# Who requests the weights: moving five of six weight loads of a recurrent layer from SyncE's queue to ScalarE's

## Chip, core and metric

The kernel runs on one core of a Trainium2 chip. The metric is the device time of one execution in microseconds (us). TensorE is called PE here, VectorE DVE, ScalarE ACT, GpSimd POOL and SyncE SP, as in the profile. Each of these engines takes its instructions from a queue of its own, in order. A DMA is requested by an instruction in one of those queues.

## The reference

The input is x, 2048 rows of 512 numbers. Each row is normalized (LN). A recurrent layer with 16 heads of 128 and an FFN with signs as weights both work on it, and one gates the other. What matters here, cut down:

```python
xn = _layernorm(x)
q = _silu(xn @ Wq); k = _silu(xn @ Wk); v = _silu(xn @ Wv); z = xn @ Wz
a = xn @ Wa; b = xn @ Wb
q, k, v = _causal_dwconv(q, conv_q_w), _causal_dwconv(k, conv_k_w), _causal_dwconv(v, conv_v_w)
q = q * cos + rot_half(q) * sin; k = k * cos + rot_half(k) * sin
q, k = (each divided by its norm, by head)
for s in range(4):                      # lags
    attn = einsum('bshd,bshd->bsh', q, lag(k, s)) * scale
    out = out + (attn * sigmoid(lag(a, s) * b))[..., None] * lag(v, s)
s = (out * rms * norm_w * _silu(z)) @ Wout
hidden = relu((xn @ sign(up).T) * up_scale)
g = _silu((hidden @ sign(down).T) * down_scale * output_scale)
return x + s * g
```

Wq, Wk, Wv and Wz are 512 x 2048, Wout is 2048 x 512, all float32. No weight stays in the chip's memory: each block of rows loads all of them again, by heads.

## The kernel before

**Tiles.** The 2048 rows are four blocks b of 512 tokens (NTB = 4), and the 16 heads are eight pairs p (NP = 8). A product (q, k, v or z of one pair in one block) multiplies a weight tile of 512 x 256 (512 KB, `load`, lines 301 to 304) with the block's transposed rows xnT, as two halves j of four matmuls each (`project`, 349 to 363). It takes 6.87 us on PE. ACT applies Silu to each half while copying it out of PSUM. `convolve` then starts with a scaling on ACT and goes on with three multiply-adds a half on DVE. The output projection takes two pairs at a time: four chunks of 128 tokens, `po`, from oz (the gated output) and wo (`output_projection`, 616 to 639).

**Steps.** `step(p, b)` (663 to 739) does the products q and k of block b + 1 and the products v and z of block b for one pair. An opening stage runs `step(p, -1)`: q and k of block 0, mixed with the first block of the FFN. Then come 24 steps with b = 0, 1 and 2, each about 35.3 us long. The last block's v and z and the other blocks' FFN follow.

**What crosses a block.** Over the pairs of a block, `sum_dots` and `sum_squares` collect the dots of q and k for each lag in PSUM. When a new block begins (p = 0, here called a change of block), `norms`, `norms_in_rows` (rows rq and rk, by SP) and `coefficients` make the factors from them. SP stores them in memory (`co_dram`) and fetches them back per pair, copied to 64 partitions a head: the tiles bc of `weighted` (569 to 605). DVE multiplies v with them (te), adds the lags up, and multiplies with z (oz, `gated_output`, line 607).

**What sets the order.** A scheduler places instructions by estimated costs, except for those issued through `pe`, `dve`, `act` or `sp`: these are proxies of class `InOrder` (68 to 78), which keep the order of the program among themselves on their engine. All their instructions bear line 76 in the profile. `nc.scalar` and `nc.sync` are free to be moved. `loads["by"]` in `load` and `load_wo` (556 to 559) is SP's queue through this stage.

**Buffers.** A pool gives a tile the slot of the tile `bufs` back, and the request for the new tile waits until the old one's readers are done. q's and k's weights take turns in three slots (pool `qks`, tag "w"), v's and z's in three others (pool `vs`), and wo in three. bc has three, oz three, PSUM's `mm` six banks.

**Where the requests stand before.** q's weight is requested at the head of `queries` (392 to 399), k's at the head of `products` (from 416), v's just ahead of its product in `step` (line 688), z's at 711 or 719 and wo's at 720. All are on SP, in one queue with the rows of x and of the norm, co_dram and bc. SP can run ahead of the products as far as the slots allow.

Of the kernel before, what the change touches and what calls it, by code (L numbers as in the profile page):

```python
# [44 lines left out]
P = 128  # L45
# [8 lines left out]
NP = H // 2  # L54
TB = 512
NTB = S // TB
# [25 lines left out]
def recurrent_layer(ctx: ExitStack, tc: tile.TileContext, a: dict, out: bass.AP):  # L82
# [3 lines left out]
    pool = InOrder(tc, nc.gpsimd)  # L86
    act = InOrder(tc, nc.scalar)

    sp = InOrder(tc, nc.sync)
    loads = {"by": nc.sync}  # L90
# [207 lines left out]

    weights = {}

    def load(pool, n, p, b):
        w = pool.tile([P, KC, 2 * P], F32, tag="w", name=f"w{n}{p}_{b}", bufs=3)
        loads["by"].dma_start(w, a[f"w{n}"][p])
        weights[n] = w

    def with_halo(pool, name, tag, bufs, p, b):

# [23 lines left out]
    def first_product(to, second_half):  # L331

        pps = [mm.tile([P, TB], F32, tag="mm", name=f"pq{j}_0_0") for j in range(2)]
        for lo in range(0, TB, TB // 2):
            for j in range(2):
                for k in range(KC):
                    pe.matmul(
                        pps[j][:, lo : lo + TB // 2],
                        weights["q"][:, k, j * P : (j + 1) * P],
                        xnT[:, k, HALO + lo : HALO + lo + TB // 2],  # L340
                        start=(k == 0),
                        stop=(k == KC - 1),
                    )
                if lo == j == 0:
                    second_half()
        for j in range(2):
            (nc.scalar if j else act).activation(to[:, j, :], pps[j], AF.Silu)

    def project(n, p, b, to):
        if n == "q" and p == b == 0:  # L350
            first_product(to, second_half)
            return
        for j in range(2):
            pp = mm.tile([P, TB], F32, tag="mm", name=f"p{n}{j}_{p}_{b}")
            for k in range(KC):
                pe.matmul(
                    pp,
                    weights[n][:, k, j * P : (j + 1) * P],
                    xnT[:, k, HALO + b * TB : HALO + (b + 1) * TB],
                    start=(k == 0),  # L360
                    stop=(k == KC - 1),
                )
            nc.scalar.activation(to[:, j, :], pp, AF.Silu)  # L363

    def raw_of(pool, n, p, b, bufs=2, raw=None):

# [24 lines left out]

    def queries(p, b):

        if p or b:
            load(qks, "q", p, b)
        q = qks.tile([P, LAGS, 2, TB], F32, tag="q", name=f"q_{p}_{b}", bufs=1)
        q0 = q[:, LAGS - 1]
        convolve(0, p, raw_of(qks, "q", p, b), q0)
        return q
# [16 lines left out]
    def products(p, b, q, between=None, beside_k=None):  # L416

        n = f"_{p}_{b}"
        if p or b:
            load(qks, "k", p, b)  # L420
        q0 = q[:, LAGS - 1]
        raw = raw_of(qks, "k", p, b)
        if p == 0:
            sum_squares(p)
        k = sum_with_halo(qks, "k", p, b)
        convolve(1, p, raw, k[:, :, HALO:])
        if between:
            between()
        turn(q)

        sq = [qks.tile([P, 2, TB], F32, tag=f"sq{j}", name=f"sq{j}" + n, bufs=3 - 2 * j) for j in range(2)]
        for j in range(2):
            act.activation(sq[j][:, 0], q0[:, j], AF.Square)
            act.activation(sq[j][:, 1], k[:, j, HALO:], AF.Square)
        nc.gpsimd.dma_start(sq[0], sq[1], accum_op=ALU.add)
        squares_due.append((p, sq[0]))
        if beside_k:
            beside_k()

        def product(to, j, lo, hi):  # L440

            k0 = k[:, j, lo : lo + TB]
            k_lags = bass.AP(k0.tensor, k0.offset, [k0.ap[0], [1, hi - lo], k0.ap[1]])
            dve.tensor_tensor(to, q[:, lo:hi, j, :], k_lags, ALU.mult)

        pr = qks.tile([P, LAGS, TB], F32, tag="pr", name="pr0" + n, bufs=2)
        product(pr, 0, 0, LAGS)
        if not b or p % 2 == 0:
            pr1 = qks.tile([P, LAGS, TB], F32, tag="pr", name="pr1" + n, bufs=2)
            product(pr1, 1, 0, LAGS)  # L450
            if b:
                nc.gpsimd.dma_start(pr, pr1, accum_op=ALU.add)
            elif p < NP - 1:
                dve.tensor_tensor(pr, pr, pr1, ALU.add)
        else:

            product(q[:, :, 1], 1, 0, LAGS)
            dve.tensor_tensor(pr, pr, q[:, :, 1], ALU.add)
        if not b:

            prs = [pr, pr1] if p == NP - 1 else [pr]
            dots_due.append([p, prs, of_head[:, p], p == NP - 1, True])
            return


        for h in range(0, P, D // 2):
            first, second = slice(h, h + D // 4), slice(h + D // 4, h + D // 2)
            if p % 2 == 0:
                nc.gpsimd.dma_start(pr[first], pr[second], accum_op=ALU.add)
            else:  # L470
                both = dots_due[-1][1][0]
                nc.gpsimd.dma_start(both[second], pr[first])
                nc.gpsimd.dma_start(both[second], pr[second], accum_op=ALU.add)
        if p % 2 == 0:
            dots_due.append([p, [pr], of_heads[:, p // 2], p == NP - 2, False])
        else:
            dots_due[-1][-1] = True
# [75 lines left out]

    wos = {}

    def load_wo(p, b):
        wo = vs.tile([P, 2, HID], F32, tag="wo", name=f"wo_{p}_{b}", bufs=3)
        loads["by"].dma_start(wo, a["wo"][p])
        wos[p] = wo

    def gates_of_output(p, b):
# [101 lines left out]
    def step(p, b, beside_q=None, beside_k=None):  # L663
# [21 lines left out]
        if z_due:  # L685
            z_due.pop()()
        if at:
            load(vs, "v", p, b)
            raw = raw_of(vs, "v", p, b, 1, rv)
        if first_due:  # L690
            first_due.pop()()
# [16 lines left out]

        early = p == 2 and b == 0
        if early:  # L710
            load(vs, "z", p, b)
            z_of()

        output_projections(strips if p % 2 == 0 or due else None)
        if change:
            coefficients(b)
        if at:
            if not early:
                load(vs, "z", p, b)
            load_wo(p, b)  # L720
            out_of = lambda: gated_output(p, b, weighted(p, b, v), z[0])
            if change:
                z_due.append(z_of)
                first_due.append(out_of)
            else:
                if not early:
                    z_of()
                out_of()
# [66 lines left out]
    with tc.tile_pool(name="pre", bufs=1, side="right") as pre:  # L795
# [64 lines left out]
        for p in range(NP):  # L860
# [9 lines left out]
            if p + 2 < NP:  # L870
                fetch(*groups[p + 2])
    vs = att.enter_context(tc.tile_pool(name="vs", bufs=1, side="right"))
    for b in range(NTB - 1):
        for p in range(NP):
            step(p, b)
# [12 lines left out]
    raw = raw_of(vs, "v", 1, last, 1)  # L888
    load(vs, "v", 2, last)
    load_wo(0, last)  # L890
    z_weights = {0: weights["z"]}
    load(vs, "z", 1, last)
    z_weights[1] = weights["z"]
    output_projections(sum_dots, 1)
    coefficients(last)
    qk.close()
# [15 lines left out]
        return up[:, f].rearrange("p (k m) -> p k m", k=KC)  # L912


    v_weights = {}
    for p in range(NP + 1):
        if 1 < p < NP:
            weights["v"] = v_weights.pop(p)
            raw = raw_of(vs, "v", p, last, 1)
        if p:  # L920
            weights["z"] = z_weights.pop(p - 1)
            z = gates_of_output(p - 1, last)
        squares_of_o()

        if p % 2 == 1 and p != 3 or p == 4:
            output_projections()
        if 1 < p < NP:
            load(vs, "z", p, last)
            z_weights[p] = weights["z"]
        if 0 < p < NP:  # L930
            v = values(p, last, raw)
        if p and p + 2 < NP:
            load(vs, "v", p + 2, last)
        if p + 2 < NP:
            v_weights[p + 2] = weights["v"]
        if p:
            gated_output(p - 1, last, o, z)
        if p < NP:
            o = weighted(p, last, v)
        if p == 4:  # L940
            load_wo(3, last)
        if 0 < p < NP and p != 3:
            load_wo(p, last)

        if p < NP:
            some = slice(2 * p, 2 * p + 2)
            pool.dma_start(up[:, some], signs_dram["up"][:, some])
        else:
            pool.dma_start(first_down, signs_dram["down"][:, 0:NFD])
        if p == 4:  # L950
            xs = in_two_terms(ffw, tokens(1), "xs", 1, [P, KC, TB], "xs1")
        elif 4 < p < 7:
            for b in range(last):
                load_squares(b, p - 5)
        elif p == NP:
            load_squares(last, 0)
            load_squares(last, 1)
# [8 lines left out]
    with tc.tile_pool(name="ff", bufs=1, side="right") as ff:  # L966
# [75 lines left out]
        for b in range(1, NTB):  # L1042
            pf = [mm.tile([P, HID], F32, tag="mm", name=f"pf{c}_{b}") for c in range(TC)]
            for f in range(2, NFC + 2):
                ub, uf = (b, f) if f < NFC else (b + 1, f - NFC)
                if uf == 0 and ub < NTB:
                    xs = ahead
                if ub < NTB:

                    ph = (mm, mm, sums, sums)[uf % 4].tile(  # L1050
# [12 lines left out]
                if b > 1 and f < 2 + TC:  # L1063
                    gate(f - 2)
                if f == NFC - 4 and b + 1 < NTB:
                    ahead = in_two_terms(
                        ff if b == 1 else ffw, tokens(b + 1), "xs", 1, [P, KC, TB], f"xs{b + 1}"
                    )
                if b == last and f >= NFC - 3:
# [105 lines left out]
```

## Time and profile before

| what | before |
|---|---|
| median of 3 timed runs | 1400.17 us (1399.67 to 1402.85) |
| the profiled execution | 1400.38 us |
| its span (first to last instruction) | 1398.6 us |
| granted TensorE clock | 0.998 |
| busy: PE / DVE / ACT / POOL | 1387.6 / 1179.3 / 671.3 / 236.1 us |
| a weight's request on SP at line 303 (32 wq, 32 wk, 24 wv, 24 wz), shortest / median | 0.327 / 0.329 to 0.384 us |
| one of 128 bc requests on SP, shortest / median / longest | 0.573 / 0.600 / 2.267 us |
| memory traffic | 263.4 MB, mean 188 GB/s |

The span is the time between the first and the last instruction in the profile. The execution's own time is 1.8 us longer. A busy time counts an engine's computing instructions; DMA requests are not in it, and stand in rows of their own (SPq is SP's queue). "Granted clock" is the share of full speed that TensorE was allowed. A wait in the profile's list of waits names the instruction that waited, and behind the arrow what ended its wait last. The opening stage ends at about 198 us, the 24 steps end at about 1018 us.

### The profile page before, as it was taken

The page shows a single profiled execution, that of the slowest core. Times are in us where ns is not written, and L with a number is a line of the kernel's source. Part 1 is how long each engine was busy: PE and PEld are TensorE (multiplying, and loading weights), DVE is VectorE, ACT ScalarE, POOL GpSimd, SP SyncE. Part 2 cuts the span into 40 slices and gives each one's busy share as a digit, 9 for nine tenths or more (in the row PEclk, how much of TensorE's full clock was granted, in tenths as well). Part 3 has the DMA queues.
Part 4 walks back from the last instruction along what each step waited for, and adds up shares of the span by engine and source line. Part 5 has one row for each costly group of instructions (what it writes and reads, how often), then busy time and mean ns, then how long its engine had stood idle before and what let it go on. Part 6 is the DMA issues. An engine that isn't in the chain of part 4 may idle for free.

```text
span 1398.6 us, 12500 instructions
## 1 busy us (share of the span) xinstructions
PE 1387.6 (99%) x3962; PEld 689.6 (49%) x3962; DVE 1179.3 (84%) x1183; ACT 671.3 (48%) x1309; POOL 236.1 (17%) x317
## 2 busy tenths in 40 slices
PE   9999999999999999999999999999999999999998
PEld 6555544444444444444444444444444444578886
DVE  7998989999898989998999999989884987337454
ACT  7566656546454564565545544545442433222122
POOL 2222111112213121113131112111111122200000
PEclk9999999999999999999999999999999999999999
DMA  9979577888988789889986897888849999654020
GB/s 315 332 171 211 129 200 166 228 203 197 231 199 186 167 167 242 212 211 196 212 186 159 171 251 186 207 181 182 176 92 207 262 233 237 142 204 136 24 90 30
DMA packets 104985, 263.40 MB, mean 188 GB/s; under 512 B 17812, under 2 KB 18324, under 8 KB 100568
## 3 DMA queue, kind: packets, MB, share of 16 engines
q0 software_dynamic: 36672, 108.02, 40.0%
q1 hardware_dynamic: 68248, 154.58, 37.1%
q8 instruction: 32, 0.52, 0.2%
q14 instruction: 33, 0.27, 0.1%
HBM read 159.77 MB, written 52.45 MB: 152 GB/s over the span
## 4 chain that ended last, share of the span: by engine, by line
PE 87%; DVE 7%; DMA 3%; ACT 1%; issue 1%; SPq 0%; DVEq 0%; ACTq 0%
PE pq L76 14%; PE pk L76 14%; PE po L76 14%; PE pz L76 13%; PE pv L76 12%; PE ph L76 8%; PE pf L76 8%; DVE q L76 2%; DVE te L76 2%; DMA wk<-in_wk_dram 1%; DVE v L76 1%; PE dots L76 1%; DMA bc<-co_dram 1%; PE squares L76 1%; DVE k L76 1%
## 5 line engine op out<-in xcount | busy, mean ns | idle before, releaser
L76 PE MATMUL pq<-xnT,wq 128*128 128x512 f32 (+1 forms) x528 | 226.1, 580 | 0.6 <-ACT rk L310 0.6
L76 PE MATMUL pk<-xnT,wk 128*128 128x512 f32 x512 | 225.3, 592 | 0.8 <-DMA wk<-in_wk_dram 0.8
L76 PE MATMUL pz<-xnT,wz 128*128 128x512 f32 x512 | 225.2, 592 | 0.5 <-ACT rv L363 0.5
L76 PE MATMUL po<-wo,oz 128*128 128x512 f32 x512 | 225.6, 595 | 0.0
L76 PE MATMUL pv<-xnT,wv 128*128 128x512 f32 x512 | 225.2, 592 | 0.0
L76 DVE TENSOR_TENSOR te<-v,bc 128x2048 f32<-128x2048 f32 x64 | 143.8, 2288 | 33.8 <-ACT v L76 15.8
L76 DVE SCALAR_TENSOR_TENSOR k<-rk,conv_w,k 128x512 f32<-128x512 f32 x192 | 141.7, 751 | 31.6 <-ACT k L375 27.1
L76 PEld LDWEIGHTS pq<-xnT,wq 128*128 128x128 f32 x528 | 99.0, 189 | 123.4 <-issue 115.1
L76 PEld LDWEIGHTS po<-wo,oz 128*128 128x128 f32 x512 | 96.2, 190 | 126.5 <-issue 117.1
L76 PEld LDWEIGHTS pz<-xnT,wz 128*128 128x128 f32 x512 | 96.6, 189 | 124.0 <-issue 119.2
L76 PEld LDWEIGHTS pv<-xnT,wv 128*128 128x128 f32 x512 | 96.6, 189 | 123.8 <-issue 120.2
L76 PEld LDWEIGHTS pk<-xnT,wk 128*128 128x128 f32 x512 | 96.5, 189 | 121.7 <-issue 119.6
L76 DVE SCALAR_TENSOR_TENSOR q<-rq,conv_w,q 128x512 f32<-128x512 f32 x192 | 141.5, 749 | 17.4 <-ACT q L375 10.6
L76 DVE SCALAR_TENSOR_TENSOR v<-rv,conv_w,v 128x512 f32<-128x512 f32 x192 | 141.3, 750 | 6.4 <-ACT v L375 1.9
L76 DVE SCALAR_TENSOR_TENSOR q<-q,turns 128x1024 f32<-128x1024 f32 (+1 forms) x128 | 127.3, 1015 | 4.9 <-ACT q L76 2.6
L76 DVE TENSOR_TENSOR pr<-q,k 128x2048 f32<-128x2048 f32 x52 | 117.3, 2287 | 0.9
L76 DVE CAST hid_hi<-hid 128x512 fp32r<-128x512 f32 x52 | 22.4, 430 | 89.7 <-ACT hid L785 89.7
L785 ACT ACTIVATE hid<-ph,up_scale 128x512 f32<-128x512 f32 x64 | 43.6, 685 | 108.6 <-PE ph L76 108.0
L363 ACT ACTIVATE rq<-pq 128x512 f32<-128x512 f32 x62 | 36.9, 596 | 98.2 <-PE pq L76 98.1
L633 ACT COPY part<-po 128x512 f32<-128x512 f32 x64 | 37.0, 580 | 87.8 <-PE po L76 87.7
L76 PE MATMUL ph<-xs_hi,up 128*128 128x512 f32 x192 | 76.8, 400 | 0.0
L76 PE MATMUL ph<-xs_lo,up 128*128 128x512 f32 x192 | 75.6, 394 | 0.0
(154 smaller groups left out, 1747.2 us busy)
## 6 DMA issues: line engine op xcount, KB each, us to landing
bc<-co_dram SPq DMA_DIRECT2D x128, 256.0 KB
pr<-pr POOLq DMA_DIRECT2D x72, 256.0 KB, 6.9
wq<-in_wq_dram SPq DMA_DIRECT2D x32, 512.0 KB
wk<-in_wk_dram SPq DMA_DIRECT2D x32, 512.0 KB
sq<-sq POOLq DMA_DIRECT2D x32, 512.0 KB, 6.7
wv<-in_wv_dram SPq DMA_DIRECT2D x32, 512.0 KB
wz<-in_wz_dram SPq DMA_DIRECT2D x32, 512.0 KB
wo<-in_wo_dram SPq DMA_DIRECT2D x32, 512.0 KB
```

Of the source, the lines that this page charges most:

```text
L76: return self.tc.keep_in_program_order(getattr(self.engine, op)(*args, **kwargs))
L363: nc.scalar.activation(to[:, j, :], pp, AF.Silu)
L633: nc.scalar.copy(part, po)
L785: nc.scalar.activation(hid, ph, AF.Relu, scale=scale)
```

## The change

The requests for q, k, v, z and wo in the 24 steps move from SP's queue to ACT's.

- The weights are kept by name, pair and block. `load` and `load_wo` take the engine that requests.
- A list, `ahead`, has all q and k weights of blocks 1 to 3 in order of use, and another all v and z weights of blocks 0 to 2. After the opening stage SP requests the first three of each.
- In `project`, after both halves of a product (and so behind its second Silu in ACT's program order), ACT requests the next of the same list. This is the weight of the product three further on in the same pool, and it goes into the slot that the product just done has left.
- wo is requested by ACT at the place in `step` where SP did it.
- The opening stage, the last block's v, z and wo, the rows of x, bc and everything else stay on SP. `ahead` at line 1066 becomes `next_xs` because the name is taken.

In the changed program PE's and DVE's instructions stand in the same order as before. SP has 114 requests fewer and ACT as many more. Some ACT instructions change places: at a change of block the squares of q and their copies come earlier, copies of halos later.

```diff
-    def load(pool, n, p, b):
+    def load(pool, n, p, b, by=None):
         w = pool.tile([P, KC, 2 * P], F32, tag="w", name=f"w{n}{p}_{b}", bufs=3)
-        loads["by"].dma_start(w, a[f"w{n}"][p])
-        weights[n] = w
+        (by or loads["by"]).dma_start(w, a[f"w{n}"][p])
+        weights[n, p, b] = w
+
+    ahead = {
+        "qk": [(n, p, b) for b in range(1, NTB) for p in range(NP) for n in "qk"],
+        "vz": [(n, p, b) for b in range(NTB - 1) for p in range(NP) for n in "vz"],
+    }
+
+    def load_ahead(pool, kind, by=None):
+        if ahead[kind]:
+            load(pool, *ahead[kind].pop(0), by)
...
     def project(n, p, b, to):
...
             nc.scalar.activation(to[:, j, :], pp, AF.Silu)
+        weights.pop((n, p, b))
+        if n in "qk" and b:
+            load_ahead(qks, "qk", act)
+        elif n in "vz" and b < NTB - 1:
+            load_ahead(vs, "vz", act)
...
     def queries(p, b):
 
-        if p or b:
+        if p and not b:
             load(qks, "q", p, b)
...
     def products(p, b, q, between=None, beside_k=None):
...
-        if p or b:
+        if p and not b:
             load(qks, "k", p, b)
...
-    def load_wo(p, b):
+    def load_wo(p, b, by=None):
         wo = vs.tile([P, 2, HID], F32, tag="wo", name=f"wo_{p}_{b}", bufs=3)
-        loads["by"].dma_start(wo, a["wo"][p])
+        (by or loads["by"]).dma_start(wo, a["wo"][p])
...
         if at:
-            load(vs, "v", p, b)
             raw = raw_of(vs, "v", p, b, 1, rv)
...
         if early:
-            load(vs, "z", p, b)
             z_of()
...
         if at:
-            if not early:
-                load(vs, "z", p, b)
-            load_wo(p, b)
+            load_wo(p, b, act)
...
     vs = att.enter_context(tc.tile_pool(name="vs", bufs=1, side="right"))
+    for _ in range(3):
+        load_ahead(vs, "vz")
+        load_ahead(qks, "qk")
     for b in range(NTB - 1):
         for p in range(NP):
             step(p, b)
```

More of the change, by code (lines that the diff above doesn't have):

```diff
@@ L338, in first_product @@
                         pps[j][:, lo : lo + TB // 2],
-                        weights["q"][:, k, j * P : (j + 1) * P],
+                        weights["q", 0, 0][:, k, j * P : (j + 1) * P],
                         xnT[:, k, HALO + lo : HALO + lo + TB // 2],
@@ L357, in project @@
                     pp,
-                    weights[n][:, k, j * P : (j + 1) * P],
+                    weights[n, p, b][:, k, j * P : (j + 1) * P],
                     xnT[:, k, HALO + b * TB : HALO + (b + 1) * TB],
@@ L890, in recurrent_layer @@
     load_wo(0, last)
-    z_weights = {0: weights["z"]}
     load(vs, "z", 1, last)
-    z_weights[1] = weights["z"]
     output_projections(sum_dots, 1)
@@ L912, in up_of @@
         return up[:, f].rearrange("p (k m) -> p k m", k=KC)
-    v_weights = {}
     for p in range(NP + 1):
         if 1 < p < NP:
-            weights["v"] = v_weights.pop(p)
             raw = raw_of(vs, "v", p, last, 1)
         if p:
-            weights["z"] = z_weights.pop(p - 1)
             z = gates_of_output(p - 1, last)
@@ L928, in recurrent_layer @@
             load(vs, "z", p, last)
-            z_weights[p] = weights["z"]
         if 0 < p < NP:
@@ L933, in recurrent_layer @@
             load(vs, "v", p + 2, last)
-        if p + 2 < NP:
-            v_weights[p + 2] = weights["v"]
         if p:
@@ L1046, in recurrent_layer @@
                 if uf == 0 and ub < NTB:
-                    xs = ahead
+                    xs = next_xs
                 if ub < NTB:
@@ L1065, in recurrent_layer @@
                 if f == NFC - 4 and b + 1 < NTB:
-                    ahead = in_two_terms(
+                    next_xs = in_two_terms(
                         ff if b == 1 else ffw, tokens(b + 1), "xs", 1, [P, KC, TB], f"xs{b + 1}"
```

## The prediction

> **What bounds the kernel now.** I read the page first: the busy times, the span in slices and the chain that ended last.
>
> ```profile
> PE 1387.6 (99%) x3962; PEld 689.6 (49%) x3962; DVE 1179.3 (84%) x1183; ACT 671.3 (48%) x1309; POOL 236.1 (17%) x317
> PE   9999999999999999999999999999999999999998
> DMA  9979577888988789889986897888849999654020
> PE 87%; DVE 7%; DMA 3%; ACT 1%; issue 1%; SPq 0%; DVEq 0%; ACTq 0%
> ```
>
> The profiled run took 1400.38 us: a span of 1398.6 and 1.8 outside it; the median of the three timed runs is 1400.17, so the two agree and I sum against 1400.4. TensorE (PE) is busy for 1387.6 us, which leaves 11.0 us idle. Next I asked what PE waited for:
>
> ```profile
> PE pf L76 <- DVE hid_lo L76: 0.9, 1, 0.9
> PE pk L76 <- DMA wk<-in_wk_dram: 0.8, 1, 0.8
> PE pq L76 <- ACT rk L310: 0.6, 1, 0.6
> PE pz L76 <- ACT rv L363: 0.5, 1, 0.5
> ```
>
> Columns: total us, times, longest. A single wait, 0.8 us, is for a weight. That row is the whole prize. The others are for the vector engines (rows of the opening stage, the last block), whose code the change leaves alone. Windows confirm it: in the stage it touches, from 195 to 1070 us, PE works 874.2 of 875 us.
>
> ```profile
> 195.00:1070.00 875.00, 874.20 (x2198) 376.01 (x2197) 806.67 (x750) 448.36 (x901) 158.15 (x198) 1.00 0.84 194
> ```
>
> Columns: length, then busy us of PE, weight load, DVE, ACT, POOL; clock, DMA share, GB/s. VectorE (DVE) is the second bound: 875 - 806.67 = 68.3 us idle over some 24.8 steps of 35.3 us, 2.75 us a step. ScalarE (ACT) is half idle. DMA works 84%.
>
> **What is removed.** SP loses 114 requests: 90 of q, k, v, z and 24 of wo. Its waits show what it does there:
>
> ```profile
> SPq L303 <- PE pq L76: 110.4, 22, 13.0
> SPq L303 <- PE pv L76: 91.3, 15, 11.6
> SPq L558 <- PE po L76: 123.3, 11, 14.5
> ```
>
> These are waits for a slot that PE is still reading. While SP stands in one, everything queued behind it on SP stands too: bc rows, x, the next weight. That is idle time of a queue, and nobody on PE's path notices but once. The one case, from SP's timeline and the chain that ended last:
>
> ```profile
> 308.40 0.33 SPq L303 DMA_DIRECT2D wk<-in_wk_dram  x1
> ```
>
> ```profile
> 308.40 20.25 DMA wk<-in_wk_dram
> 328.79 7.11 PE pk L76 x16
> ```
>
> The weight of pair 4, block 1 was requested at 308.40, landed 20.25 us later, and PE started 0.8 us late. After the change ACT requests it behind the second Silu of the product three back in its pool, pq of pair 3; in ACT's timeline that Silu ends at 301.15, some 7 us sooner. If the weight takes as long again, it lands at about 321.4, ahead of 328.0, when PE wanted it. **-0.8 us.**
>
> Here the skill speaks against any gain: "DMA: Bandwidth & Descriptors", section "Issuing engines are not separate DMA queues", says that DMAs from scalar, sync and gpsimd share the same 16 engines, so that issuing from several saves only the time to initiate, usually small. By that rule the gain is one issue, 0.33 us, and 0.5 of the wait remains. By the row it is the earlier slot, not the issue, and all 0.8 goes. I take the row; the ends are 0.3 and 0.8.
>
> The same number of buffers (three to a pool) limits the lead before and after. Elsewhere weights land at least 4.6 us ahead of their product, so being earlier there is worth nothing. At nothing too stand SP's six requests at the start of the stage, the keyed dictionary and the renaming; PE's and DVE's instruction orders are identical, POOL's differs by a few neighbours.
>
> **What is added on ACT.** 114 requests, 4.75 a step. No ACT-issued DMA is in the trace. SP's own rows bound it: a weight's request takes 0.33 us alone, about 0.55 after others, and 1.4 to 2.5 under backlog (2.54 for wq at 315.34). Below zero it cannot be. I take 0.55, as ACT's requests come one at a time, with 63 us in all; ACT's share in the stage goes from 51% to 58%. A request also waits for its slot and for the DMA eight back in the two queues' shared set of completion semaphores (the built program shows these waits); nearly always both are past by then. The slot is the product's own reads, done before its Silu.
>
> Queued behind each q, k or v request is the scaling that opens the same product's convolution, and DVE waits for that. The DVE waits "k <- ACT k" are 27.1 us in 15 times and "q <- ACT q" 10.6 in 7 in the whole span, so DVE is up against ACT in about one product in four. If all three requests of a step were on DVE's path, they would cost 3 x 0.55 = 1.65 us, inside the 2.75 that it has. Behind DVE stands PE: PSUM banks are freed by ACT's Silu some 8 to 19 us before PE needs them (typically 16), so 0.55 there is nothing. wo's request waits on po of the step before last, also past. **In the ordinary steps: 0.**
>
> If that cover is gone, the thin places are where po needs the last oz: 2.4 us at 279.4, 2.3 at 344.3, and, thinnest, at the two later changes of block: 1.04 us at 557.7 (oz ends at 556.67, po's third matmul starts 555.99 + 4 x 0.43) and 1.42 at 841.8. There DVE runs without a gap for over 20 us:
>
> ```profile
> 547.26 4.49 DVE L76 TENSOR_TENSOR te<-v,bc 128x2048 f32<-128x2048 f32 x2 [0.18 <-ACT xnT L76]
> 551.79 2.29 DVE L76 TENSOR_TENSOR te<-te,te 128x2048 f32<-128x2048 f32 x1
> 555.45 1.22 DVE L76 TENSOR_TENSOR oz<-te,z 128x1024 f32<-128x1024 f32 x1
> ```
>
> te waits for ACT's square (0.18), and the change puts three requests (v, z, q) ahead of that square: 3 x 0.55 = 1.65 less the 0.5 or so that ACT idles ahead of them, 1.2 us later. In return ACT's new order has the other squares earlier and some halo copies later, and lets DVE start 0.7 to 0.85 sooner (my reading of the order against the durations). Net 0.4 later, inside 1.04.
>
> **What else meets at these changes.** SP's queue before:
>
> ```profile
> 511.51 0.33 SPq L539 DMA_DIRECT2D co_dram<-rk  x1
> 519.04 7.59 SPq L76 DMA_DIRECT2D bc<-co_dram  x6
> 526.67 1.41 SPq L303 DMA_DIRECT2D wv<-in_wv_dram  x1
> ```
>
> bc (the coefficients) goes first and three weights follow it. After, ACT requests them behind their products, the first two at about 517 and 524 (as their Silus ran), beside bc. bc has 2.9 us in hand before its te in the first of these changes and 1.4 in the second (landing against te's start). Of before, no row shows a weight on a second queue beside bc. The skill, "DMA: Bandwidth & Descriptors", section "Queues, rings and completion order": each DMA engine takes turns between the queues that have work, a packet at a time. By this rule two weights, 1 MB at some 225 GB/s, put bc back 4.7 us: 1.8 and 3.3 over the margin, less PE's 1.04 and 1.42, is 0.8 + 1.9 = 2.7 us. By the rows one weight is down before bc starts (512 KB take 4 to 6 us there) and one is beside it: 2.3 us, which the first change swallows and of which the second passes on 0.9, less than 1.42. co_dram has one wo instead of two ahead of it and lands 1 to 2 us sooner. Ends: 0 and 2.7; nearer the row, **+0.3 at each of the two, +0.6**.
>
> **Sum.** 1400.4 - 0.8 + 0.6 = **1400.2 us**. No change that can be measured: 0.2%, 2.8 us, is about what a measurement of this kernel can tell.
>
> **Rivals.**
> *The weights were the limit.* For it: the 0.8 us row, and SP's hundreds of us in waits for slots. Against: all that PE waits for in the stage is that row. Even with 0.5 of the last block, 1400.4 - 1.3 = 1399.1. Chance 0.12.
>
> *The change doesn't move what it says.* The slots are as many as before, so the weight could land late again behind the traffic: 0.8 stays, and so does all else: 1400.4 to 1401. Chance 0.08.
>
> *Coefficients late (slower).* Place: the changes of block at 535 and 817. Weights from ACT's queue take turns with bc. Price: if bc lands 5 us late at both, (5 - 2.9 - 1.0) + (5 - 1.4 - 1.4) = 3.3, and with the later square, 0.4 each, about 4: 1404. It decides from 3.9 us late at the first and 2.8 at the second. For it: DMA share 0.99 in 510 to 545. Against: co_dram comes sooner. Chance 0.16.
>
> *ACT is held by its requests (slower).* If a request holds ACT for over 0.9 us, three of them exceed DVE's 2.75 a step and the lag accumulates until po waits. At 1.5 us, with one step in two up against ACT: (4.5 - 2.75) / 2 x 21 = 18 at worst; since DVE meets ACT in a quarter of the products only, I price it at 6: 1406. For it: SP's rows of 1.4 to 2.5. Against: SP's were back to back, ACT's are 7 us apart. Chance 0.16.
>
> **How the numbers follow.** The forecast has 0.48: 1399.4 to 1402. Slower by over 0.2% (above 1403): nearly all of the fourth rival, two thirds of the third, and 0.05 of the forecast's own tail: 0.31. Faster (under 1397.4): more than the whole idle time of the stage, so only a mis-read of the tail: 0.03. Same: 0.66. Range 1398.8 to 1406.0: it leaves out the far end of the two slow rivals.
>
> **What would show it.** Right: PE's wait for wk gone; ACT's rows of requests near 0.55 us and its busy share up by some 6 points if issues were counted; DVE's waits for ACT up by under 1.65 us a step; PE in 195 to 1070 within 1 us of full; new PE waits, if any, at po near 557 and 841 and under 1 us. Wrong: "te <- DMA bc" in DVE's waits (third rival); DVE's waits for ACT's k, q and v up by tens of us with PE waits at po in every second step (fourth); or PE waits for weights in places that had none.

## The result, and the profile after

The changed kernel is slower: 1407.54 us at the median of 6 runs (1405.63 to 1409.37), against 1401.59 for the kernel before in 6 runs (1399.67 to 1403.38). The ratio is 1.0045, with a 95% interval from 1.0031 to 1.0059, some 6 us. The profiled execution took 1406.85 us, its span is 1405.1.

The view that answers to the list of PE's waits:

```profile
PE dots L76 <- issue: 2.8, 1, 2.8
PE po L76 <- DVE oz L76: 1.6, 3, 0.9
...
PE pf L76 <- DVE hid_lo L76: 1.2, 2, 0.9
```

The wait for wk (0.8 us) is gone, as forecast. In its place stand one wait of 2.8 us at the dots, whose releaser this view can't name, and three small ones for oz. Laying PE's stream after beside that of before, group by group, shows where the distance grows: PE is 1.2 us late at 349.6, 4.2 at the dots behind it, 5.9 at the product behind those (358.4), and it stays between 5.6 and 6.5 to the end. Nearly all is lost within 15 us, in the step of pair 4, block 0. PE's timeline there, before and then after (start, length, instruction, times; in brackets the idle time ahead of it):

```profile
342.60 7.03 PE L76 MATMUL po<-wo,oz 128*128 128x512 f32 x16
349.56 1.06 PE L76 MATMUL squares<-sq,of_head 128*32 128x512 f32 x8
350.44 1.04 PE L76 MATMUL dots<-pr,of_heads 128*32 128x512 f32 x8
351.42 7.13 PE L76 MATMUL po<-wo,oz 128*128 128x512 f32 x16
```

```profile
342.67 1.88 PE L76 MATMUL po<-wo,oz 128*128 128x512 f32 x4
345.43 5.42 PE L76 MATMUL po<-wo,oz 128*128 128x512 f32 x12 [0.88 <-DVE oz L76]
350.78 1.07 PE L76 MATMUL squares<-sq,of_head 128*32 128x512 f32 x8
354.64 1.25 PE L76 MATMUL dots<-pr,of_heads 128*32 128x512 f32 x8 [2.79 <-issue]
355.82 8.59 PE L76 MATMUL po<-wo,oz 128*128 128x512 f32 x16
```

Three losses stand in it. PE waits 0.88 us for oz. It waits 2.79 at the dots. And the po that follows takes 8.59 us instead of 7.13, though it waits for nothing: 1.46 us. The windows show why; the column after the five engines is the granted clock:

```profile
350.00:355.00 5.00, 2.21 (x14) 0.36 (x17) 4.86 (x8) 4.38 (x9) 5.00 (x6) 1.00 1.03 258
355.00:360.00 5.00, 5.00 (x15) 1.91 (x8) 4.89 (x4) 0.08 (x1) 1.01 (x2) 0.66 1.10 231
360.00:365.00 5.00, 5.00 (x13) 2.24 (x12) 4.93 (x6) 1.14 (x2) 1.73 (x2) 1.00 1.11 196
```

After its two idle spells PE lost clock: 0.66 is the mean of the 5 us from 355. A narrower window shows half the clock:

```profile
355.50:358.50 3.00, 3.00 (x7) 1.18 (x4) 2.90 (x4) 0.00 (x0) 0.64 (x1) 0.50 1.13 240
```

By half-microsecond windows (0.88 from 355 to 355.5, 0.71 from 358.5 to 359, full outside) the half clock lasted some 3.4 us. The page's own clock strip, whose slices are 35 us long, hides that.

**What the dots waited for.** The chain that ended last, followed through that window, names it:

```profile
337.34 15.31 DMA pr<-pr
352.65 1.99 issue
354.64 1.25 PE dots L76 x8
```

The dots of pairs 2 and 3 need four adds on the DMA queue of POOL (pr onto pr, 256 KB each). In the kernel before the last two were requested at 335.72 and 339.74 and landed at 347.81 and 349.20, 1.24 us ahead of the dots. After the change they were requested at 337.34 and 338.32, the last even earlier, and landed at 352.65 and 354.55: they took 15 to 16 us.

**What held the adds.** The DMA view from 338 to 348 us, kernel before and then changed:

```profile
DMA packets 665, 1.78 MB, mean 178 GB/s; under 512 B 118, under 2 KB 118, under 8 KB 601
```

```profile
DMA packets 136, 0.29 MB, mean 29 GB/s; under 512 B 9, under 2 KB 9, under 8 KB 136
```

For ten microseconds the DMA engines move almost nothing, while two adds, two coefficient loads and two weights are waiting. What stands just ahead is a store of 2 KB, the negated means of block 2 (`centre`, line 238), cut into 512 pieces of 4 bytes. SP's row for it, before and after:

```profile
331.48 0.38 SPq L238 DMA_DIRECT2D ln_dram<-ln  x1
```

```profile
336.36 0.38 SPq L238 DMA_DIRECT2D ln_dram<-ln  x1
```

When it landed is told by POOL's adds to x, which wait for it (before, then after):

```profile
342.59 0.90 POOL L241 DMA_DIRECT2D xnT<-ln_dram  x1 [2.07 <-DMA ln_dram<-ln]
348.29 0.90 POOL L241 DMA_DIRECT2D xnT<-ln_dram  x1 [9.19 <-DMA ln_dram<-ln]
```

It takes 10.8 us to land before and 11.7 after. Before, it was requested 4.2 us ahead of the third add; after, one. So the hole, from about 333 to 340 us before and from 338 to 348 after, moved onto the adds. Before, only the third add was requested into its tail (it took 12.1 us, the last one 9.5).

**Why the store came 4.9 us later.** Two parts, read from ACT's timeline. Before:

```profile
330.92 0.20 ACT L76 ACTIVATE mv<-sums 128x1 f32<-128x1 f32 x1
331.15 0.20 ACT L76 ACTIVATE sums<-sums 128x1 f32<-128x1 f32 x1
331.26 0.19 ACT L234 ACTIVATE ln<-mv 128x4 f32<-128x4 f32 x1
332.63 0.20 ACT L310 COPY rv<-kept_rv 128x6 f32<-128x6 f32 x1 [1.18 <-DVE v L76]
```

After:

```profile
334.58 0.19 ACT L76 ACTIVATE mv<-sums 128x1 f32<-128x1 f32 x1
335.94 0.20 ACT L322 COPY rv<-kept_rv 128x6 f32<-128x6 f32 x1 [1.17 <-DVE v L76]
336.04 0.20 ACT L76 ACTIVATE sums<-sums 128x1 f32<-128x1 f32 x1
336.14 0.19 ACT L234 ACTIVATE ln<-mv 128x4 f32<-128x4 f32 x1
```

The scheduler has put a copy that waits for DVE (rv's halo) ahead of `ln<-mv`, which the store needs: 1.57 us. The other 3.31 are DVE's own lateness, which ACT inherits. Some 0.35 us of it dates from the opening stage. The rest DVE gathered at three places of the first change of block: 0.55 us where k's scaling on ACT came later (207.93 instead of 207.03), 1.0 where it waited for the last of the eight row copies, which landed at about 232.5 instead of 228.0, and 1.58 at te of pair 1:

```profile
273.16 2.29 DVE L76 TENSOR_TENSOR te<-v,bc 128x2048 f32<-128x2048 f32 x1 [1.50 <-DMA o_dram<-te]
```

te's buffer was still being read by POOL's store of the squares of pair 0; it took 9.0 us instead of 7.3. Three weights on ACT's queue (wo's among them) were requested beside it, but experiments 10 and 11 below, where SP requests, have stores of 9.8 and 9.5 us at this place.

**What ACT's requests cost.** In the changed kernel's rows of wk:

```profile
L76 ACTq DMA_DIRECT2D wk<-in_wk_dram x23: 334/334/392, 199.6 to 974.4; - x23
L303 SPq DMA_DIRECT2D wk<-in_wk_dram x9: 328/328/4803, 3.6 to 177.2; - x9
```

```profile
206.32 0.60 ACT L375 ACTIVATE rk<-pk 128x512 f32<-128x512 f32 x1 [1.78 <-PE pk L76]
206.38 0.34 ACTq L76 DMA_DIRECT2D wq<-in_wq_dram  x1
206.95 0.20 ACT L327 COPY kept_rk<-rk 128x6 f32<-128x6 f32 x1
```

A request takes 0.334 us, and it runs while the Silu ahead of it is still being executed. The next instruction starts 0.03 us behind the Silu, as it did before the change (206.57, then 206.60). The request itself costs ACT nothing here; the 0.55 us at k came from another copy (of the squares, 0.58 us) that the new order put ahead of k's.

### The profile page after: what moved, and what is told of

Read it like the earlier page. It is cut to its first block, busy times and chain, and to the rows that moved or that the text cites. A ratio compares the mean times of both kernels' runs of the same rounds, so it can differ in the third digit from the quotient of the medians.

```text
span 1405.1 us, 12414 instructions
## 1 busy us (share of the span) xinstructions
PE 1391.1 (99%) x3962; PEld 690.9 (49%) x3962; DVE 1179.4 (84%) x1183; ACT 666.7 (47%) x1309; POOL 235.9 (17%) x317
## 4 chain that ended last, share of the span: by engine, by line
PE 79%; DVE 9%; DMA 6%; issue 4%; ACT 1%; POOL 0%; SPq 0%; ACTq 0%; DVEq 0%; POOLq 0%
PE pq L76 13%; PE pz L76 13%; PE pk L76 12%; PE po L76 12%; PE pv L76 12%; PE pf L76 7%; PE ph L76 7%; DVE q L76 3%; DVE te L76 2%; DMA pr<-pr 2%; DVE k L76 2%; PE dots L76 1%; DVE pr L76 1%; DVE v L76 1%; DMA ln_dram<-ln 1%
```

## The experiments

Twelve kernels, each timed against the kernel before in five rounds. In the first four the theory was only that the loss begins at the first change of block, and the rivals were the cost of a request on ACT and the new order as such.

**1. The new order on SP's queue.**

```diff
-            load_ahead(qks, "qk", act)
+            load_ahead(qks, "qk")
...
-            load_ahead(vs, "vz", act)
+            load_ahead(vs, "vz")
...
-            load_wo(p, b, act)
+            load_wo(p, b)
```

> The weights are requested in the changed order, three products ahead, but all by SP's queue; ACT requests none. Theory (the loss comes from ACT's requests landing beside, and ahead of, rows and adds at the first change of block, which make DVE 3.3 us late between 207 and 273 us): with one queue in order again, DVE is less than 1 us late there, and the time is within 2 us of the kernel before, ratio about 1.000 (0.9995 to 1.0015). Rival 1 (the new order of the requests costs, whoever makes them): about 6 us slower, ratio 1.0045. Rival 2 (114 requests hold ACT): as the kernel before, ratio 1.000, but then the runs with fewer ACT requests must gain in proportion.

Measured: 1460.77 us, ratio 1.0431 (1.0412 to 1.0451). Every expectation missed. Its waits say why, first SP's, then DVE's:

```profile
SPq L575 <- PE po L76: 191.9, 19, 27.1
SPq L303 <- PE pk L76: 154.4, 26, 15.1
```

```profile
DVE te L76 <- DMA bc<-co_dram: 105.8, 16, 16.3
```

SP stands in waits for slots with the coefficients queued behind it. The early order is only bearable on a queue of its own. (PE waits 1.7 us at the dots near 350 here too, without a request on ACT; the store of means went out at 332.79.) So two of the next kernels, which put part of this order on SP, test SP's queue as much as their own question.

**2. wo back on SP.** Only `load_wo(p, b, act)` becomes `load_wo(p, b)`.

> The changed kernel with wo's 24 requests back on SP. Theory: wo of pair 1 no longer lands beside the store of squares that te of pair 1 waits for at 270 us; of DVE's 3.3 us of lateness about 1 goes, 2.3 stay; ratio 1.002 to 1.004. Rival 2 (each of 114 requests costs the same on ACT): 24 of 114 fewer, 1.3 us back, ratio 1.0036. Rival 3 (wo alone is the cause): ratio 1.000.

Measured: 1405.85 us at the median of six runs, of which one (3784 us) is disturbed and not in the ratio: 1.0031 (1.0018 to 1.0044). te of pair 1 is 2.77 us late instead of 3.31, and the dots wait 2.16. The interval covers both the theory's range and rival 2's figure, and overlaps the changed kernel's. It excludes rival 3 only.

**3 and 4. Four steps on SP, the rest on ACT; and the reverse.** The requests take `by = act` only outside, or only inside, the steps of pairs 0 to 3 in block 0.

> The changed kernel, but the requests made in the first four steps (block 0, pairs 0 to 3) are SP's; all later ones ACT's. Theory (all is lost at the first change of block): DVE on time at 273 us, no PE wait at po and dots near 345 to 355 us, ratio 0.9995 to 1.001. Rival 2 (ACT is held by each request): some 20 of 114 requests fewer, 1 us back, ratio 1.0038.

> The other half: ACT requests in the first four steps only, SP in all later ones. Theory: the whole loss stays, ratio 1.004 (1.003 to 1.005), with DVE 3 us late at 273 us and PE waiting at the dots near 354 us. Rival 2: 20 of 114 requests, 1 us, ratio 1.0008.

Measured: 1413.51 us, ratio 1.0091 (1.0078 to 1.0105), and 1459.13, ratio 1.042 (1.0399 to 1.0441). Both are misses: each stretch that SP requests three ahead loses as in experiment 1 (in the first of them PE waits 8.8 us for an oz near 415 us). So neither ratio says anything of ACT. Their first 355 us do bear on what follows. In the first kernel DVE is 2.6 us late at te all the same, but SP, held up by coefficients, sends the store of means only at 346.65, behind the adds. The dots don't wait:

```profile
350.94 1.04 PE L76 MATMUL dots<-pr,of_heads 128*32 128x512 f32 x8
```

In the reverse kernel the store goes out at 335.47, and the dots wait 1.6 us, as was expected of it.

**5. Block 0 as before, ACT from then on, first attempt.** The weights of pairs 0 to 6 are requested on demand, where the kernel before does it.

> In block 0 (pairs 0 to 6) the weights are requested where and when the kernel before does it, by SP, and only then by ACT as in the changed kernel. Theory (all is lost in block 0): DVE as before at 273 us, no PE wait above 1 us at 345 to 355 us; ratio 1.000 (0.999 to 1.001). Rival 2 (each ACT request costs): 75 of 114 remain, 4 us, ratio 1.003. Rival 4 (the later changes of block, at 558 and 842 us, lose as soon as PE is not already late): PE waits at po there of 1 to 3 us, ratio 1.001 to 1.003.

Measured: 1622.63 us, ratio 1.1539 (1.1505 to 1.1574). The list of requests could not run ahead of the ones on demand, so ACT's lead after block 0 was one product, not three:

```profile
PE pk L76 <- DMA wk<-in_wk_dram: 96.7, 17, 10.6
PE pz L76 <- DMA wz<-in_wz_dram: 46.4, 9, 9.9
```

k's weight is now requested behind the product of q, just when its own product should start (443.95 the first time), and PE waits for it up to 10.6 us. Up to 443 us, though, where block 0's requests are SP's as before, its PE stream follows the kernel before within 0.2 us, dots included.

**6. One request later.** k's weight of pair 2 is requested one product later, away from the row copies:

```diff
-            load_ahead(qks, "qk", act)
+            if (n, p, b) != ("q", 1, 1):
+                load_ahead(qks, "qk", act)
+            if (n, p, b) == ("k", 1, 1):
+                load_ahead(qks, "qk", act)
```

> The changed kernel, with one request moved: the weight of k of pair 2, block 1 is requested with the next one, one product later (some 230 instead of 222.7 us), and so no longer beside the eight row copies rq and rk. Theory: the last row lands near 228 instead of 231.9, DVE's rk is 1 us earlier, DVE 2.3 instead of 3.3 us late at 273; ratio 1.002 to 1.004. If this wait is not on the path: 1.0045 unchanged.

Measured: 1409.38 us, ratio 1.0044 (1.003 to 1.0058). DVE's rk no longer waits and starts 1.5 us earlier, but at te DVE is 2.84 instead of 3.31 us late, and the dots wait 2.7 all the same. This wait is not what decides.

**7 and 8. No store of pair 0's squares; and both edits.**

```diff
+            if p == b == 0:
+                return
-            if p == 0:
+            if p == (0 if b else 1):
                 pool.dma_start(o2_dram[b], o2)
```

> The changed kernel without the store of the squares of pair 0 in block 0 (its part is missing from the norm of o in that block; pair 1 stores in its place instead of adding). te of pair 1, at 270 us, then has no store to wait for. Theory: DVE 1.8 instead of 3.3 us late at 273; the wait at oz near 345 goes, the one at the dots near 354 shrinks; ratio 1.001 to 1.003.

> Both edits together (later request of one weight of k, no store of the squares of pair 0 in block 0). Theory: DVE is under 1 us late at 273 us, as much as the order on ACT costs; no PE wait at oz near 345, at most 1 us at the dots; ratio 0.9995 to 1.0015. Rival 2 (ACT's requests as such): still 1.004.

Measured: 1408.64 us, ratio 1.0033 (1.0019 to 1.0047), and 1407.18, ratio 1.0027 (1.0017 to 1.0038). The theory in its first form (DVE's lateness as such) falls here. DVE's lateness at te is halved (1.5 and 1.6 us), the wait for oz near 345 is gone, and the dots still wait, 3.9 and 3.1 us. In both the store of means goes out at 334.6, and the last add lands at 353.9 and 353.1. So I looked at what the adds stand behind, and formed the theory of the small store.

**9 and 10. The same store in 16-byte pieces.** For the statistics only, the rows of x are assigned to partitions in another order, so that a partition's four means lie side by side in memory:

```diff
-        nc.sync.dma_start(x_in, a["x"][t * P : (t + 1) * P, :])
+        nc.sync.dma_start(x_in, a["x"][b * TB : (b + 1) * TB, :].rearrange("(p c) h -> c p h", c=TC)[c])
...
-            nc.sync.dma_start(ln_dram[b][i].rearrange("(c p) -> p c", p=P), ln[:, i, :])
+            nc.sync.dma_start(ln_dram[b][i].rearrange("(p c) -> p c", p=P), ln[:, i, :])
```

> The changed kernel; only the layout of the two small stores of block 2's and 3's mean and deviation changes: 128 pieces of 16 bytes instead of 512 of 4, with the rows of x for these statistics loaded in the matching order. All engines keep their order. Revised theory (most of the loss is the wait for the dots near 354 us: that store comes 4.9 us later than before, so that the last two adds of the products pr, requested at 337 and 338, stand behind its 10 us instead of the tail of it): the adds land before 348, no wait at the dots, no lower clock after it; DVE is still 3.3 us late and the 0.9 at oz near 345 stays; ratio 1.0005 to 1.002. If the adds are late for the traffic of weights alone: 1.0045 unchanged.

> The kernel before with the same layout of these stores: a control. Theory: PE waited for nothing there but 0.8 us for one weight, so at most that is won; ratio 0.999 to 1.000. If it gains over 3 us, the stores cost something of their own elsewhere.

Measured: changed kernel 1401.33 us, ratio 1.0000 (0.9992 to 1.0008); kernel before 1401.65, ratio 0.9995 (0.9986 to 1.0004). The orders on all engines are those of the kernel each comes from. With it the changed kernel loses nothing that can be measured, which is better than the range expected of it, and the kernel before gains nothing. The edited changed kernel's PE near the dots:

```profile
344.77 5.42 PE L76 MATMUL po<-wo,oz 128*128 128x512 f32 x12 [0.89 <-DVE oz L76]
350.12 1.06 PE L76 MATMUL squares<-sq,of_head 128*32 128x512 f32 x8
351.00 1.04 PE L76 MATMUL dots<-pr,of_heads 128*32 128x512 f32 x8
351.97 7.13 PE L76 MATMUL po<-wo,oz 128*128 128x512 f32 x16
```

Its DVE is still 2.6 us late at te, its store still goes out late (335.70), the 0.89 at oz is still there. But the store lands in 4.0 us, the DMA engines are busy from 338 to 348,

```profile
DMA packets 842, 2.14 MB, mean 214 GB/s; under 512 B 130, under 2 KB 130, under 8 KB 778
```

the adds land at 344.9 and 348.0, the dots don't wait, and the clock stays up. (Its profiled execution, 1405.38 us, is the slowest of its 14 runs; it is 0.8 us behind the kernel before at 1090 us and loses the rest in the FFN, which the edit doesn't touch.) This shows the cause: much was late in the changed kernel, but what PE paid for was the small store's hole over the adds.

The edit also spaces the rows of x's loads otherwise, and no kernel has one without the other. The traces speak against the loads as the cause. In the changed kernel, loads of x are requested at 232.02 and 262.88, and the engines move 240 and 221 GB/s from 233 to 239 and from 263 to 269. The second small store (block 2's deviations, requested at 377.46 and 376.80) has the same hole in the changed kernel and none with the edit:

```profile
379.00:388.00 9.00, 9.00 (x23) 3.96 (x22) 3.99 (x6) 7.22 (x14) 2.50 (x3) 1.00 0.19 8
```

```profile
378.00:388.00 10.00, 10.00 (x24) 4.37 (x24) 8.47 (x13) 8.89 (x19) 0.00 (x0) 1.00 1.01 245
```

A store in 4-byte pieces need not leave a hole: behind the same one in the kernel before (374.16) the engines move 190 GB/s from 376 to 386. Why not there is open.

**11. Block 0 as before, ACT from then on, with three in hand.**

> In block 0 (pairs 0 to 6) the weights are requested by SP where the kernel before does it, with three in hand at the change to ACT, and from then on by ACT three products ahead. (An earlier kernel of this kind had only one product of lead after block 0 and is no test of this.) Theory (all is lost in block 0): ratio 1.000 (0.999 to 1.0015). Rival 2 (each ACT request costs): 1.003. Rival 4 (the later changes of block lose when PE is not already late): 1.001 to 1.003, with waits at po near 558 and 842 us.

Measured: 1402.89 us, ratio 1.0006 (0.9995 to 1.0017). ACT's requests in blocks 1 and 2 cost nothing that can be measured. Its profiled execution (1405.75 us, above its median) is instructive all the same:

```profile
PE dots L76 <- issue: 2.2, 1, 2.2
...
PE po L76 <- DVE oz L76: 1.3, 3, 0.7
```

There, with SP requesting and `ln<-mv` ahead of rv's copy, te of pair 1 still waited for the store of squares (1.9 us late), the store of means went out at 333.41, and the dots waited 2.2. So a store 1.9 us later is enough to bring the wait on. As the median of 19 runs shows no loss, most executions of this kernel probably don't have it; only this one was profiled.

**12. The store later.** ACT's `ln<-mv` of block 2 is kept in program order (`act` for `nc.scalar` at line 234).

> The changed kernel with ACT's negated mean of block 2, which the first of the two small stores waits for, kept in program order, and so later, behind the adds of pr instead of ahead of them. Revised theory: the adds land early, no wait at the dots near 354; the 0.9 at oz stays; ratio 1.0005 to 1.002, unless something else then stands behind the store. If the store is not what holds the adds: 1.0045.

Measured: 1412.83 us, ratio 1.0078 (1.0066 to 1.009), a miss in the time. The first half came true: the adds of pairs 2 and 3 land at 344.1 and 345.6 and their dots don't wait. The next dots do:

```profile
PE dots L76 <- DMA pr<-pr: 6.4, 1, 6.4
```

The stores of means and of deviations go out at 377.9 and 380.0, and the adds of pairs 4 and 5 are requested at 401 to 422 instead of 398 to 403. While the first two of them are under way there is no hole: the engines move 284 GB/s from 400 to 420 us. POOL's four adds to x, which need the means, went out just ahead (397.77), and so did an add of squares. That these held the others is the likely reading, but was not tried. Sending the store later is no cure by itself.

## Why the prediction was wrong, step by step

The window of before that counts is the stretch behind the first change of block, where DVE (third of the engines) is busy 68.3 of 70 us:

```profile
275.00:345.00 70.00, 69.20 (x173) 29.77 (x172) 68.32 (x65) 41.15 (x87) 12.68 (x18) 1.00 0.79 190
```

- **PE's wait for wk, -0.8 us: came true, but not by the earlier slot alone.** In the changed kernel the weight is requested at 302.38 instead of 308.40, and the wait is gone. It is gone as well in experiments 10 and 11, where SP requests this weight even later (310.09 and 309.61).
- **A request on ACT, 0.55 us taken, 63 us in all: too high.** It is 0.334 us, and hidden under ACT's running instruction. The fourth rival (ACT held by its requests) is refuted by experiment 9, where ACT makes all 114 and nothing is lost, and by experiment 11. ACT did stand behind requests that waited for another DMA's completion (twice for over 5 us in its waits), contrary to "nearly always both are past", but no PE wait came of it.
- **The two later changes of block, +0.6 us: the right size.** In the changed kernel, whose PE is late by then, PE waits at neither. In experiment 11 it waits 0.7 us for oz at 845 and not near 558, in experiment 6 1.5 at the same place; experiment 10, the kernel before with the other layout, has 0.5 near 558. A thin place near 700, which the list lacks, cost 0.25 in the changed kernel and 1.3 in experiment 6. The third rival's late coefficients did not happen: te waits for bc once in the whole span, 13.7 us, against 14.9 before.
- **"In the ordinary steps: 0": the step that failed.** I carried DVE's lateness only to the later changes of block. I left out the first one, behind which DVE is nearly full for 70 us. The 2.75 us a step that I took for DVE's slack are a mean; these two steps have 0.8 each. I listed the thin places as po behind oz only. The dots behind POOL's adds had 1.24 us to spare in the trace of before, less than any but one in that list, and were not in it. Their price was 2.8 us, and that of the lowered clock behind them 1.46. The two listed places at 279.4 and 344.3 cost 0.49 and 0.88 us of waiting.
- **The mechanism was in none of the rivals.** A store of 2 KB that PE never waits for, at a time set by ACT and DVE, was priced at nothing. The trace of before has the same hole (69 GB/s from 335 to 340.5 us), nearly over when the last add was requested (339.74). After the change the store came 4.9 us later, and the hole lay over the last two adds.
- **ACT's new order as a gain of 0.7 to 0.85 us: wrong in sign where it mattered.** By the trace it cost 0.55 us at k and 1.57 at the store.

The sum, as PE's stream shows it: 0.3 in the opening (not of the change), oz at 280 and 345 1.9, wk -1.0, the dots 3.0 and 0.2 behind them, the clock 1.5, oz at 705 0.5, -0.8 in the last block and +0.8 in the FFN: together 6.4.

With the store in larger pieces the move of the requests is worth nothing (1.0000 against 0.9995, experiments 9 and 10). So the Trainium skill, "DMA: Bandwidth & Descriptors", section "Issuing engines are not separate DMA queues", is borne out for the whole kernel where it says that issuing from several engines saves only the time to initiate. It does not speak of the queue's order, which made experiment 1 lose 4.3%.

The lowered clock, by PE's idle spells near 345 and 354 and the mean clock from 355 to 360: 0.30 and 2.25 us (experiment 11), clock 1.00; 0.89 and 2.16 (experiment 2), 1.00; 3.06 in one (experiment 8), 1.00; 0.89 and 2.69 (experiment 6), 0.79, with 0.50 from about 354 to 357; 0.88 and 2.79 (the changed kernel), 0.66; 3.91 in one (experiment 7), 0.66. The rows of experiments 8 and 7:

```profile
355.00:360.00 5.00, 5.00 (x13) 2.23 (x12) 4.93 (x4) 0.59 (x1) 0.86 (x1) 1.00 1.10 212
```

```profile
355.00:360.00 5.00, 5.00 (x11) 2.21 (x9) 4.93 (x4) 0.00 (x0) 0.29 (x1) 0.66 1.05 198
```

The Trainium skill, "TensorE: Matmul & The Clock Gate", section "What's actually happening", gives a free-running window of about 3.4 us: after an idle one the array gets half its clock, after a busy one the full clock. The half clock and its length, 0.50 for some 3.4 us, agree. The onset does not: spells of 2.69 and 2.79 us, each with 0.9 us some 7 us earlier, were enough here, which one wholly idle window of 3.4 us would not give. Whether the shorter spell mattered is not shown.

**What stays open.** How much of the store's 4.9 us is due to the order on ACT and how much to the weights' landing beside rows and squares has been read from the trace (1.57 and 3.31) and not tried apart. te's wait for the store of squares appears, 1.8 and 1.5 us, also in experiments 10 (kernel before) and 11, where SP requests in block 0, so it isn't the ACT requests' alone. And what makes the engines idle behind the store's small pieces, some times and not others, is not shown.

## What to carry to other kernels

Where an engine is 99% busy, list every input with less than some 3 us to spare, DMAs between memories included, and not only those that the edit touches; then ask what a lag of 2 to 3 us would push onto them. Look for stores in pieces of a few bytes: the bottleneck may never wait for them, and yet wait for what is requested behind them. And read the order that the scheduler makes of the instructions that were not moved: by the trace, that cost more here than the 114 requests that were.

## What the runs showed of the hardware

- Behind a store of 512 pieces of 4 bytes (2 KB) the DMA engines moved 29 GB/s for ten microseconds with requests waiting, and 8 GB/s for nine behind a second; behind one of the same kind in the kernel before they moved 190. The same 2 KB in 128 pieces of 16 bytes landed in 4.0 us, and the stretch of the first moved 214 GB/s.
- A DMA request on ACT's queue took 0.334 us at the median, and in the rows above it ran beside ACT's instruction ahead of it.
- Waits of 2.8 us and of 0.9 within ten microseconds cost PE another 1.46 us: its clock fell to 0.50 for some 3.4 us. After 3.06 us in one wait it did not fall.
- The same order of early requests cost 4.3% on SP's queue, in front of the coefficients, and 0.45% on ACT's.
